# The last stage of a two-layer graph kernel: written order, output in dead buffers, seven input buffers

## The chip, the cores and the metric

The kernel runs on one core of one Trainium2 chip. The metric is device time in microseconds (us) of one execution. The kernel before takes 2909.42 us (median of three runs, 2908.18 to 2910.81); the profiled execution spans 2908.0 us. The engines are called by the names the profile gives them: PE is the matrix engine (PEld its weight loads), DVE the vector engine, ACT the scalar engine, POOL is GpSimd, SP the engine that here only issues transfers. A batch means one of the 16 slices of the input, 1024 rows of 256 numbers, 1 MB in float32.

## The reference, cut to what matters

Two layers, each of which adds the output of a graph network to its input and normalises every row. Only the end of layer 1 is touched.

```python
def _layernorm(x, axis=-1, eps=1e-5):
    m = jnp.mean(x, axis=axis, keepdims=True)
    v = jnp.var(x, axis=axis, keepdims=True)
    return (x - m) / jnp.sqrt(v + eps)

def _L1_gnn_ref(features, A, W1, b1, g1, be1, W2, b2, g2, be2):
    # ... A_hat = the normalised adjacency
    agg = jnp.einsum('nm,bmd->bnd', A_hat, features)
    x = agg.reshape(-1, d)
    h = jax.nn.relu(_batchnorm(x @ W1.T + b1, g1, be1))
    out = h @ W2.T + b2
    out = _batchnorm(out, g2, be2)      # statistics over all 16 x 1024 rows, per feature
    return out.reshape(b, n, -1)

# x: (16, 1024, 256), float32
x = _layernorm(x + _L0_gnn_ref(x, ...), axis=-1)      # layer 0, not touched here
x = _layernorm(x + _L1_gnn_ref(x, adj, ...), axis=-1) # layer 1
```

The second batch norm needs statistics over all batches, so nothing of the last stage can start until the last matrix product with `W2` has been measured. The stage then does, for every batch: scale and shift each feature, transpose back from feature-major to row-major, add the input of the layer (called x1), take mean and variance of each row, normalise, store.

## The kernel before

The stage before the last one computes `h @ W2.T` for every batch and keeps all 16 results in SBUF, feature-major, in the tiles `o2T` (128 features x 2 x 1024 rows). x1 was written to DRAM by layer 0 and is read back into the tiles `xf`, of which there are three (`fin`, `bufs=3`). The tiles `hl` (two of 2 MB) hold the operand of the product.

```python
ps_t = ctx.enter_context(tc.tile_pool(name="ps_t", bufs=2, space=PSUM))   # tile_t: 128 x 512
ps_o = ctx.enter_context(tc.tile_pool(name="ps_o", bufs=2, space=PSUM))   # tile_o: 128 x 512
mhalf = const.tile([P, NCH], F32, name="mhalf")                           # all -0.5

def rsqrt(dst, src, eps):                       # lines 577 and 579
    n = dst.shape[1]
    if eps:
        nc.gpsimd.tensor_scalar(dst, src, eps, None, ALU.add)
        src = dst
    nc.gpsimd.tensor_tensor(dst, src, mhalf[:, :n], ALU.pow)
# ... cut: layer 0 and the first part of layer 1
with (
    tc.tile_pool(name="o2p", bufs=1) as o2p,
    tc.tile_pool(name="fin", bufs=3) as fin,
):
    o2T = [o2p.tile([P, CC, N], F32, tag=f"o2_{b}", name=f"o2_{b}") for b in range(B)]
    xf = {}
    def load_x1(b):                             # transfer at line 1086
        xf[b] = fin.tile([P, NCH, C], F32, tag="xf", name=f"xf_{b}")
        nc.sync.dma_start(xf[b], x1_d[b])

    with tc.tile_pool(name="hl", bufs=2) as hl:
        # ... cut: per batch, load hl, relu and scale on ACT, product into o2T (lines 1092 to 1107),
        #     bn_stats of o2T into bn2_st (line 1111)
            if b >= B - 3:
                load_x1(b - (B - 3))            # x1 of batches 0, 1, 2

    sg2, sh2 = batchnorm_coeffs(bn2_st, cols["g2"], cols["be2"], CC, "bn2")

    def residual2(b):
        for c in range(CC):                     # CC = 2
            o = o2T[b][:, c, :]
            nc.scalar.activation(o, o, AF.Identity, bias=sh2[:, c : c + 1],
                                 scale=sg2[:, c : c + 1])            # line 1123
        xt = xf[b]
        st = small.tile([P, NCH, 6], F32, tag="ln_st", name=f"st_l1_{b}")
        mv = small.tile([P, NCH, 2], F32, tag="ln_mv", name=f"mv_l1_{b}")
        for pair in range(NCH // 2):            # NCH = 8
            pt = tile_t(f"pf_{b}_{pair}")
            for j in range(2):
                n = 2 * pair + j
                for c in range(CC):
                    nc.tensor.transpose(
                        pt[:, j * C + c * P : j * C + (c + 1) * P],
                        o2T[b][:, c, n * P : (n + 1) * P], ident)    # line 1134
            xs = xt[:, 2 * pair : 2 * pair + 2, :].rearrange("p n c -> p (n c)")
            nc.vector.tensor_add(xs, pt, xs)                         # line 1139
            for n in (2 * pair, 2 * pair + 1):
                nc.vector.bn_stats(st[:, n, :], xt[:, n, :])         # line 1141
                nc.vector.bn_aggr(mv[:, n, :], st[:, n, :])          # line 1142
        rstd = small.tile([P, NCH], F32, tag="ln_rs", name=f"rs_l1_{b}")
        rsqrt(rstd, mv[:, :, 1], EPS)
        nmr = small.tile([P, NCH], F32, tag="ln_nm", name=f"nm_l1_{b}")
        nc.vector.scalar_tensor_tensor(nmr, mv[:, :, 0], -1.0, rstd,
                                       op0=ALU.mult, op1=ALU.mult)   # line 1146
        return rstd, nmr

    def finish(b, rstd, nmr):
        xt = xf.pop(b)
        for n in range(NCH):
            nc.scalar.activation(xt[:, n, :], xt[:, n, :], AF.Identity,
                bias=nmr[:, n : n + 1], scale=rstd[:, n : n + 1])    # line 1154
        nc.gpsimd.dma_start(out[b].rearrange("(n p) c -> p n c", p=P), xt)  # line 1158

    before = None
    for b in range(B):
        if b not in xf:
            load_x1(b)
        now = residual2(b)
        if before is not None:
            finish(b - 1, *before)
        before = now
    finish(B - 1, *before)
```

Within an engine the compiler's scheduler chooses the order of these instructions. In the kernel before, ACT does the scaling of batches 0 to 4 in one row, then the first normalisation, and so on.

Of the kernel before, what the change touches and what calls it, by code (L numbers as in the profile page):

```python
# [10 lines left out]
F32 = mybir.dt.float32  # L11
I32 = mybir.dt.int32
AF = mybir.ActivationFunctionType
ALU = mybir.AluOpType
# [4 lines left out]
P = 128  # L19
HALF = 512  # L20
EPS = 1e-5
# [494 lines left out]
def fast_path(  # L516
# [19 lines left out]
    nc = tc.nc  # L536
    B, N, C = x.shape
    H = 4
    D = C // H
    NCH = N // P  # L540
    CC = C // P
    FH = W1.shape[0]
    HC = FH // P
    scale = float((1.0 + 1e-06) / (np.sqrt(D) + 1e-06))

    const = ctx.enter_context(tc.tile_pool(name="const", bufs=1))
    small = ctx.enter_context(tc.tile_pool(name="small", bufs=4))
# [5 lines left out]
    def tile_s(name):  # L553
        return ps_s.tile([P, N], F32, tag="s", name=name)

    def tile_t(name):
        return ps_t.tile([P, HALF], F32, tag="t", name=name)

    def tile_o(name):
        return ps_o.tile([P, HALF], F32, tag="o", name=name)  # L560
# [6 lines left out]
    ident = const.tile([P, P], F32, name="ident")  # L567
# [3 lines left out]
    mhalf = const.tile([P, NCH], F32, name="mhalf")  # L571
    nc.gpsimd.memset(mhalf, -0.5)

    def rsqrt(dst, src, eps):
# [5 lines that stand above are left out]
# [33 lines left out]
    with (  # L613
# [15 lines left out]
        st = {}  # L629
# [242 lines left out]
        with tc.manual_schedule(engines={mybir.EngineType.PE, mybir.EngineType.Activation, mybir.EngineType.DVE}):  # L872
# [25 lines left out]
            for j in range(len(bursts)):  # L898
                b, u = j // PERB, j % PERB
# [28 lines left out]
            j = len(bursts)  # L928
# [38 lines left out]
    with (  # L967
# [34 lines left out]
        for m in range(NCH):  # L1002
            for half in range(2):
                pt = tile_t(f"pah_{m}_{half}")
# [53 lines left out]
    def batchnorm_coeffs(stats, gamma, beta, k, name):  # L1058

        mv = const.tile([P, k, 2], F32, name=f"{name}_mv")  # L1060
        sg = const.tile([P, k], F32, name=f"{name}_sg")
        sh = const.tile([P, k], F32, name=f"{name}_sh")
        for j in range(k):
            nc.vector.bn_aggr(mv[:, j, :], stats[:, j].rearrange("p a s -> p (a s)"))
        rsqrt(sg, mv[:, :, 1], EPS)
        nc.vector.tensor_mul(sg, sg, gamma)
        nc.vector.tensor_mul(sh, mv[:, :, 0], sg)
        nc.vector.tensor_sub(sh, beta, sh)
        return sg, sh
# [5 lines left out]
# [4 lines that stand above are left out]
        o2T = [  # L1079
            o2p.tile([P, CC, N], F32, tag=f"o2_{b}", name=f"o2_{b}") for b in range(B)  # L1080
        ]
        xf = {}

        def load_x1(b):
            xf[b] = fin.tile([P, NCH, C], F32, tag="xf", name=f"xf_{b}")
            nc.sync.dma_start(xf[b], x1_d[b])

        with tc.tile_pool(name="hl", bufs=2) as hl:
            sg1, sh1 = batchnorm_coeffs(bn1_st, cols["g1"], cols["be1"], HC, "bn1")
            for b in range(B):  # L1090
                ht = hl.tile([P, HC, N], F32, tag="hl", name=f"hl_{b}")
                nc.sync.dma_start(ht, h_d[b])
                for k in range(HC):
                    nc.scalar.activation(  # L1094
                        ht[:, k, :], ht[:, k, :], AF.Relu,
                        bias=sh1[:, k : k + 1], scale=sg1[:, k : k + 1],
                    )
                for c in range(CC):
                    ps = tile_s(f"po2_{b}_{c}")
                    for k in range(HC):  # L1100
                        for half in range(2):
                            hs = slice(half * HALF, (half + 1) * HALF)
                            nc.tensor.matmul(  # L1103
                                ps[:, hs], w2T[:, k, c * P : (c + 1) * P], ht[:, k, hs],
                                start=(k == 0), stop=(k == HC - 1),
                            )
                    nc.vector.tensor_scalar(
                        o2T[b][:, c, :], ps, cols["b2"][:, c : c + 1], None, ALU.add
                    )
                    for half in range(2):  # L1110
                        nc.vector.bn_stats(
                            bn2_st[:, c, 2 * b + half, :],
                            o2T[b][:, c, half * HALF : (half + 1) * HALF],
                        )
                if b >= B - 3:
                    load_x1(b - (B - 3))

        sg2, sh2 = batchnorm_coeffs(bn2_st, cols["g2"], cols["be2"], CC, "bn2")

        def residual2(b):  # L1120
            for c in range(CC):
                o = o2T[b][:, c, :]
                nc.scalar.activation(
                    o, o, AF.Identity, bias=sh2[:, c : c + 1], scale=sg2[:, c : c + 1]
                )
            xt = xf[b]
            st = small.tile([P, NCH, 6], F32, tag="ln_st", name=f"st_l1_{b}")
            mv = small.tile([P, NCH, 2], F32, tag="ln_mv", name=f"mv_l1_{b}")
            for pair in range(NCH // 2):
                pt = tile_t(f"pf_{b}_{pair}")  # L1130
                for j in range(2):
                    n = 2 * pair + j
                    for c in range(CC):
                        nc.tensor.transpose(
                            pt[:, j * C + c * P : j * C + (c + 1) * P],
                            o2T[b][:, c, n * P : (n + 1) * P], ident,
                        )
                xs = xt[:, 2 * pair : 2 * pair + 2, :].rearrange("p n c -> p (n c)")
                nc.vector.tensor_add(xs, pt, xs)
                for n in (2 * pair, 2 * pair + 1):  # L1140
                    nc.vector.bn_stats(st[:, n, :], xt[:, n, :])
                    nc.vector.bn_aggr(mv[:, n, :], st[:, n, :])
            rstd = small.tile([P, NCH], F32, tag="ln_rs", name=f"rs_l1_{b}")
            rsqrt(rstd, mv[:, :, 1], EPS)
            nmr = small.tile([P, NCH], F32, tag="ln_nm", name=f"nm_l1_{b}")
            nc.vector.scalar_tensor_tensor(
                nmr, mv[:, :, 0], -1.0, rstd, op0=ALU.mult, op1=ALU.mult
            )
            return rstd, nmr

        def finish(b, rstd, nmr):
            xt = xf.pop(b)
            for n in range(NCH):
                nc.scalar.activation(  # L1154
                    xt[:, n, :], xt[:, n, :], AF.Identity,
                    bias=nmr[:, n : n + 1], scale=rstd[:, n : n + 1],
                )
            nc.gpsimd.dma_start(out[b].rearrange("(n p) c -> p n c", p=P), xt)  # L1158

        before = None  # L1160
        for b in range(B):
            if b not in xf:
                load_x1(b)
            now = residual2(b)
            if before is not None:
                finish(b - 1, *before)
            before = now
        finish(B - 1, *before)

def kernel(tc: tile.TileContext, *args):


    with tc.tile_pool(name="flag", bufs=1, space=DRAM) as flag:
        good_d = flag.tile([1, 1], I32, name="good_d")
        fast_path(tc, *args, good_d)
        good = tc.nc.values_load(good_d[0:1, 0:1], min_val=0, max_val=2 * P)  # L1179
        with tc.If(good < 2 * P):  # L1180
            general_path(tc, *args)
# [30 lines left out]
```

## Time and profile before

| what | value |
|---|---|
| time, median of three | 2909.42 us |
| span of the profiled execution | 2908.0 us |
| last matrix product ends, last statistics | about 2743 us |
| first scaling of the last stage on ACT (line 1123) | 2745.93 us |
| last normalisation on ACT (line 1154) begins, its 8 instructions take | 2895.33 us, 4.04 us |
| end of span | 2908.0 us |
| store of one batch (line 1158), median from issue to landing | 5.6 us |
| transfers in the last stage | 13 loads of x1 and 16 stores, 1024 KB each |

The profile gives the start of an instruction or of a run of like instructions ("x8"), how long it ran, and in brackets how long its engine sat idle before it and what ended that idle time ("<-DMA xf<-x" is the arrival of an x1 load). A table by stretches gives, for each engine, busy time and in brackets the number of instructions, then the clock that the matrix engine was granted, the busy share of the 16 transfer engines and the rate they moved.

### The profile page before, as it was taken

Reading aid. Unit: us, or ns where it says so; the run is one execution under the profiler, and the core shown is the slowest. Engines: PE = TensorE matmul, PEld = TensorE weight load, DVE = VectorE, ACT = ScalarE, POOL = GpSimd, SP = SyncE. Lnnn points to the kernel's source line nnn. Section 1 sums busy time; section 2 is a strip of 40 time slices with the busy share of each in tenths; the row PEclk is TensorE's granted clock in tenths of the full one; section 3 lists DMA queues with packets and bytes.
Section 4 is the critical chain, followed back from the end, with each engine's and each line's share of the span. In section 5 each row is a group of like instructions: output and inputs, shape, how many; then the busy total and the mean of one; then the engine's idle time right before and its main releaser. Section 6 shows DMA issues by size and latency. Waiting matters only on the chain. (4 is left out here: it accounts for less than half of the span.)

```text
span 2908.0 us, 32691 instructions
## 1 busy us (share of the span) xinstructions
PE 2702.1 (93%) x13522; PEld 1200.7 (41%) x13522; DVE 1444.5 (50%) x2130; ACT 1138.5 (39%) x1313; POOL 185.8 (6%) x196
## 2 busy tenths in 40 slices
PE   5899999999999999999999998799999999999842
PEld 2344443444444444444443446444444444344332
DVE  2456666656656756765765655411112112333464
ACT  2444644554553653653563542010111001233473
POOL 0000000000000000100000001000000000000032
PEclk8899999999999999999999997799999999999955
DMA  4001011011011101101101011022121111334165
GB/s 130 8 8 30 9 37 30 9 36 38 16 23 37 30 9 37 30 8 37 30 9 38 16 51 39 15 87 116 72 87 68 76 73 58 130 145 161 70 222 199
DMA packets 122062, 169.00 MB, mean 58 GB/s; under 512 B 86704, under 2 KB 103600, under 8 KB 111664
## 3 DMA queue, kind: packets, MB, share of 16 engines
q1 hardware_dynamic: 112720, 99.70, 11.3%
q0 software_dynamic: 9184, 67.12, 5.9%
q8 instruction: 108, 1.77, 0.3%
q14 instruction: 50, 0.41, 0.0%
HBM read 99.36 MB, written 67.44 MB: 57 GB/s over the span
## 5 line engine op out<-in xcount | busy, mean ns | idle before, releaser
L779 ACT ACTIVATE p<-ps 128x1024 f32<-128x1024 f32 x512 | 495.0, 1019 | 151.9 <-PE ps L774 82.8
L774 PE MATMUL ps<-qT,kT 64*64 64x512 f32 x4096 | 496.4, 599 | 12.1 <-ACT p L779 12.1
L795 PE MATMUL po<-p,v 64*64 64x512 f32 x4096 | 486.9, 589 | 0.0
L804 DVE TENSOR_TENSOR acc<-acc,p 128x1024 f32<-128x1024 f32 x384 | 469.9, 1224 | 26.0 <-ACT p L779 3.5
L700 PE MATMUL pg<-wg,x 128*128 128x512 f32 x1024 | 451.4, 594 | 1.6 <-ACT kT L721 1.6
L1024 PE MATMUL pagg<-ahT,x1l 128*128 128x512 f32 x1024 | 444.1, 593 | 0.0
L1043 ACT ACTIVATE hw<-ph,col_b 128x1024 f32<-128x1024 f32 x64 | 71.3, 1114 | 657.1 <-PE ph L1039 657.1
L1024 PEld LDWEIGHTS pagg<-ahT,x1l 128*128 128x128 f32 x1024 | 194.4, 191 | 241.1 <-issue 241.1
L700 PEld LDWEIGHTS pg<-wg,x 128*128 128x128 f32 x1024 | 189.7, 190 | 231.9 <-issue 216.5
L795 PEld LDWEIGHTS po<-p,v 64*64 64x64 f32 x4096 | 162.6, 133 | 277.8 <-issue 277.1
L774 PEld LDWEIGHTS ps<-qT,kT 64*64 64x64 f32 x4096 | 148.9, 133 | 299.9 <-issue 225.8
L709 ACT ACTIVATE qT<-qT 128x512 f32<-128x512 f32 x64 | 40.4, 631 | 529.8 <-DVE qT L706 529.8
L1103 PE MATMUL po<-hl,w2T 128*128 128x512 f32 x512 | 222.8, 598 | 6.9 <-ACT hl L1094 6.9
L1028 DVE COPY agg<-pagg 128x1024 f32<-128x1024 f32 x32 | 39.2, 1225 | 377.8 <-PE pagg L1024 377.8
L1039 PE MATMUL ph<-agg,w1T 128*128 128x512 f32 x512 | 222.2, 592 | 0.0
L688 DVE SCALAR_TENSOR_TENSOR wg<-wg,adj_s 128x1024 f32<-128x1024 f32 x128 | 170.9, 1353 | 50.1 <-ACT wg L684 50.1
L706 DVE SCALAR_TENSOR_TENSOR qT<-pg,para_s 128x512 f32<-128x512 f32 x64 | 44.2, 690 | 259.5 <-PE pg L700 259.5
L850 POOL TENSOR_TENSOR x<-x,o 128x512 f32<-128x512 f32 x64 | 81.0, 1266 | 1418.3 <-DVE o L845 1418.3
L730 PE MATMUL pv<-kvw_s,xT 128*128 128x256 f32 x512 | 127.0, 393 | 35.3 <-DVE v L734 25.5
L1045 DVE BATCH_NORM_STATS2 bn_st<-hw 128x6 f32<-128x512 f32 x128 | 82.4, 685 | 152.3 <-ACT hw L1043 152.3
L679 ACT ACTIVATE wg<-crow,ccol 128x1024 f32<-128x1024 f32 x128 | 147.4, 1151 | 16.7 <-DMA crow<-c 16.6
L1103 PEld LDWEIGHTS po<-hl,w2T 128*128 128x128 f32 x512 | 98.3, 192 | 131.4 <-issue 121.9
(87 smaller groups left out, 2034.9 us busy)
## 6 DMA issues: line engine op xcount, KB each, us to landing
h<-hw POOLq DMA_DIRECT2D x16, 2048.0 KB, 6.6
hl<-h SPq DMA_DIRECT2D x16, 2048.0 KB
x<-in_x_dram SPq DMA_DIRECT2D x16, 1024.0 KB
x<-x POOLq DMA_DIRECT2D x16, 1024.0 KB, 4.2
x1l<-x SPq DMA_DIRECT2D x16, 1024.0 KB
xf<-x SPq DMA_DIRECT2D x16, 1024.0 KB
out_dram<-xf POOLq DMA_DIRECT2D x16, 1024.0 KB, 5.6
crow<-c SPq DMA_DIRECT2D x16, 512.0 KB
```

Source lines behind the costliest of these rows:

```text
L679: nc.scalar.activation(w, s["crow"], AF.Abs, bias=s["ccol"][:, n : n + 1])
L688: nc.vector.scalar_tensor_tensor(w, w, 1.0, adj_s[:, n, :], op0=ALU.subtract, op1=ALU.mult)
L700: nc.tensor.matmul(ps, xt[:, n, c * P : (c + 1) * P], s["wg", n][:, hs], start=(n == 0), stop=(n == NCH - 1),)
L730: nc.tensor.matmul(pt[:, j * C : (j + 1) * C], s["xT"][:, c, n * P : (n + 1) * P], kvw_s[:, c, C : 2 * C], start=(c == 0), stop=(c == CC - 1),
L774: nc.tensor.matmul(ps[kh * D : (kh + 1) * D, hd * HALF : (hd + 1) * HALF], kT[r, pr, ks], qT[r, pr, qh * HALF : (qh + 1) * HALF], start=Tr ...
L779: nc.scalar.activation(p, ps, AF.Exp)
L795: nc.tensor.matmul(g["po"][kh][hd * D : (hd + 1) * D, :], s["v"][r, m, h * D : (h + 1) * D], p[r, hd * HALF : (hd + 1) * HALF], start=(m = ...
L804: nc.vector.tensor_add(g["acc"], g["acc"], p)
L1024: nc.tensor.matmul(ps[:, hs], xt[:, m, c * P : (c + 1) * P], ahT[:, m, hs], start=(m == 0), stop=(m == NCH - 1),)
L1039: nc.tensor.matmul(ps[:, hs], w1T[:, c, k * P : (k + 1) * P], t[:, c, hs], start=(c == 0), stop=(c == CC - 1),)
L1045: nc.vector.bn_stats(bn1_st[:, k, 2 * b + half, :], ht[:, k, half * HALF : (half + 1) * HALF])
L1103: nc.tensor.matmul(ps[:, hs], w2T[:, k, c * P : (c + 1) * P], ht[:, k, hs], start=(k == 0), stop=(k == HC - 1),)
```

## The change

Four things are changed, all in the last stage. First, PE, ACT and DVE follow the order of the program text there (`manual_schedule`), and the text is arranged so that the scaling of a batch comes a batch ahead of its use. Second, the normalised rows are written into `o2T[b]`, which nobody reads any more once the batch has been transposed, and not in place; the store reads from there, and is issued on SP. So an `xf` tile comes free when the normalisation has read it, not when the store has landed. Third, there are four more `xf` tiles (`fin2`), in the space that `hl` leaves, seven in all. Fourth, the mean and variance are no longer put together by `bn_aggr` on DVE: ten small GpSimd instructions on all eight row groups at once compute the two coefficients from the raw statistics (even and odd elements have mean and summed square deviation each). The transposes use both pairs of PSUM tiles in turn.

```diff
-        def load_x1(b):
-            xf[b] = fin.tile([P, NCH, C], F32, tag="xf", name=f"xf_{b}")
+        def load_x1(b, pool):
+            xf[b] = pool.tile([P, NCH, C], F32, tag="xf", name=f"xf_{b}")
             nc.sync.dma_start(xf[b], x1_d[b])
 ... cut
+        with (
+            tc.tile_pool(name="fin2", bufs=4) as fin2,
+            tc.manual_schedule(
+                engines={mybir.EngineType.PE, mybir.EngineType.Activation, mybir.EngineType.DVE}
+            ),
+        ):
+            for b in range(3, 7):
+                load_x1(b, fin2)
+            def scale_shift(b):
+                for c in range(CC):
+                    o = o2T[b][:, c, :]
+                    nc.scalar.activation(
+                        o, o, AF.Identity, bias=sh2[:, c : c + 1], scale=sg2[:, c : c + 1]
+                    )
             def residual2(b):                      # scaling taken out of it
-                pt = tile_t(f"pf_{b}_{pair}")
+                pt = tile_t(f"pf_{b}_{pair}") if pair % 2 else tile_o(f"pf_{b}_{pair}")
                 ... transposes, tensor_add, bn_stats as before
-                    nc.vector.bn_aggr(mv[:, n, :], st[:, n, :])
-            rsqrt(rstd, mv[:, :, 1], EPS)
-            nc.vector.scalar_tensor_tensor(
-                nmr, mv[:, :, 0], -1.0, rstd, op0=ALU.mult, op1=ALU.mult
-            )
+                me, qe, mo, qo = (st[:, :, k] for k in (1, 2, 4, 5))
+                w = small.tile([P, 4, NCH], F32, tag="ln_w", name=f"w_l1_{b}")
+                rstd, nmr, dif, var = (w[:, k, :] for k in range(4))
+                pool = nc.gpsimd
+                pool.tensor_tensor(nmr, me, mo, ALU.add)
+                pool.tensor_tensor(dif, me, mo, ALU.subtract)
+                pool.tensor_tensor(var, qe, qo, ALU.add)
+                pool.tensor_scalar(var, var, 1.0 / C, EPS, ALU.mult, ALU.add)
+                pool.tensor_tensor(dif, dif, dif, ALU.mult)
+                pool.tensor_scalar(dif, dif, 0.25, None, ALU.mult)
+                pool.tensor_tensor(var, var, dif, ALU.add)
+                pool.tensor_tensor(rstd, var, mhalf, ALU.pow)
+                pool.tensor_tensor(nmr, nmr, rstd, ALU.mult)
+                pool.tensor_scalar(nmr, nmr, -0.5, None, ALU.mult)
+                return rstd, nmr
             def finish(b, rstd, nmr):
                 xt = xf.pop(b)
+                y = o2T[b].rearrange("p c n -> p (c n)").rearrange("p (n c) -> p n c", c=C)
                 for n in range(NCH):
                     nc.scalar.activation(
-                        xt[:, n, :], xt[:, n, :], AF.Identity,
+                        y[:, n, :], xt[:, n, :], AF.Identity,
                         bias=nmr[:, n : n + 1], scale=rstd[:, n : n + 1],
                     )
-            nc.gpsimd.dma_start(out[b].rearrange("(n p) c -> p n c", p=P), xt)
+                nc.sync.dma_start(out[b].rearrange("(n p) c -> p n c", p=P), y)
+                if b + 7 < B:
+                    load_x1(b + 7, fin if b < 3 else (fin2 if b < 7 else fin))
+            scale_shift(0)
+            coeffs = {}
+            for b in range(B):
+                coeffs[b] = residual2(b)
+                if b + 1 < B:
+                    scale_shift(b + 1)
+                if b:
+                    finish(b - 1, *coeffs.pop(b - 1))
+            finish(B - 1, *coeffs.pop(B - 1))
```

In the compiled program the instructions of every engine are in the same order as before up to this stage. In it, ACT's order is scaling of 0, 1, 2, normalisation of 0, scaling of 3, normalisation of 1, and so on to scaling of 15, normalisation of 13, 14, 15. The loads of x1 for batches 3 to 6 wait on PE and ACT (the last use of `hl`), and each later load stands on SP behind the store of the batch whose buffer it takes.

More of the change, by code (lines that the diff above doesn't have):

```diff
@@ L1115, in fast_path @@
                 if b >= B - 3:
-                    load_x1(b - (B - 3))
+                    load_x1(b - (B - 3), fin)
         sg2, sh2 = batchnorm_coeffs(bn2_st, cols["g2"], cols["be2"], CC, "bn2")
[L1120 to L1124, printed above, removed]
-                )
[L1126 to L1129, printed above, removed]
-                pt = tile_t(f"pf_{b}_{pair}")
[L1131 to L1143, printed above, removed]
-            rsqrt(rstd, mv[:, :, 1], EPS)
-            nmr = small.tile([P, NCH], F32, tag="ln_nm", name=f"nm_l1_{b}")
-            nc.vector.scalar_tensor_tensor(
-                nmr, mv[:, :, 0], -1.0, rstd, op0=ALU.mult, op1=ALU.mult
-            )
-            return rstd, nmr
@@ L1151, in finish @@
[L1151 to L1154, printed above, removed]
-                    xt[:, n, :], xt[:, n, :], AF.Identity,
[L1156 to L1167, printed above, removed]
@@ L1168, in fast_path, with residual2, finish @@
-        finish(B - 1, *before)
+        with (
[12 more added lines that the diff above has]
+                    )
+            def residual2(b):
+                xt = xf[b]
+                st = small.tile([P, NCH, 6], F32, tag="ln_st", name=f"st_l1_{b}")
+                for pair in range(NCH // 2):
+                    pt = tile_t(f"pf_{b}_{pair}") if pair % 2 else tile_o(f"pf_{b}_{pair}")
+                    for j in range(2):
+                        n = 2 * pair + j
+                        for c in range(CC):
+                            nc.tensor.transpose(
+                                pt[:, j * C + c * P : j * C + (c + 1) * P],
+                                o2T[b][:, c, n * P : (n + 1) * P], ident,
+                            )
+                    xs = xt[:, 2 * pair : 2 * pair + 2, :].rearrange("p n c -> p (n c)")
+                    nc.vector.tensor_add(xs, pt, xs)
+                    for n in (2 * pair, 2 * pair + 1):
+                        nc.vector.bn_stats(st[:, n, :], xt[:, n, :])
+                me, qe, mo, qo = (st[:, :, k] for k in (1, 2, 4, 5))
[13 more added lines that the diff above has]
+                return rstd, nmr
+            def finish(b, rstd, nmr):
+                xt = xf.pop(b)
+                y = o2T[b].rearrange("p c n -> p (c n)").rearrange("p (n c) -> p n c", c=C)
+                for n in range(NCH):
+                    nc.scalar.activation(
+                        y[:, n, :], xt[:, n, :], AF.Identity,
+                        bias=nmr[:, n : n + 1], scale=rstd[:, n : n + 1],
+                    )
+                nc.sync.dma_start(out[b].rearrange("(n p) c -> p n c", p=P), y)
[10 more added lines that the diff above has]
+            finish(B - 1, *coeffs.pop(B - 1))
```

## The prediction

> **What bounds the kernel now.** The slices of the page show PE at nine tenths nearly throughout; only in the last stage (after 2745) is it half idle. So I cut that stage into stretches of 10 us, to see whether any engine is full:
>
> ```profile
> core 0: us, PE busy (x) PEld busy (x) DVE busy (x) ACT busy (x) POOL busy (x), PEclk, DMA share, GB/s
> 2765.00:2775.00 10.00, 3.82 (x16) 3.14 (x16) 5.68 (x21) 10.00 (x19) 3.54 (x5) 0.50 0.73 265
> 2775.00:2785.00 10.00, 3.08 (x14) 2.61 (x14) 5.04 (x18) 8.40 (x13) 2.63 (x4) 0.50 0.90 324
> 2815.00:2825.00 10.00, 4.64 (x20) 3.47 (x18) 6.76 (x27) 4.58 (x9) 1.90 (x2) 0.50 0.69 245
> 2845.00:2855.00 10.00, 2.51 (x11) 2.14 (x12) 4.32 (x15) 2.71 (x6) 1.91 (x2) 0.50 0.56 219
> ```
>
> ACT is full early, while it runs ahead with scaling. From 2815 on no engine is full, and the transfers aren't either. The stage waits; the order of time says for what (start, length, engine, line; in brackets the idle time before):
>
> ```profile
> 2835.99 4.04 ACT L1154 ACTIVATE xf<-xf,nm_l,rs_l 128x256 f32<-128x256 f32 x8 [4.56 <-issue]
> 2840.34 0.96 POOL L1158 DMA_DIRECT2D out_dram<-xf  x1 [4.63 <-ACT xf L1154]
> 2841.60 5.10 SPq L1086 DMA_DIRECT2D xf<-x  x2
> ...
> 2849.13 0.69 DVE L1139 TENSOR_TENSOR xf<-pf,xf 128x512 f32<-128x512 f32 x1 [4.61 <-DMA xf<-x]
> ...
> 2850.01 0.23 POOL L577 TENSOR_SCALAR rs_l<-mv_l 128x8 f32<-128x8 f32 x1 [8.72 <-DVE mv_l L1142]
> 2850.33 1.67 POOL L579 TENSOR_TENSOR rs_l<-rs_l,mhalf 128x8 f32<-128x8 f32 x1
> 2852.04 0.17 DVE L1146 SCALAR_TENSOR_TENSOR nm_l<-mv_l,rs_l 128x8 f32<-128x8 f32 x1 [1.55 <-POOL rs_l L579]
> ```
>
> Two things. A load of x1 is issued at 2841.60 and its add starts at 2849.13: with three tiles a load waits for a store to land, so normalise, store, load, add stand in one ring. And POOL waits 8.72 us for the means of a batch whose adds were over at 2843: in the scheduler's order its last `bn_aggr` stands behind the first add of the next batch, and so behind that load. ACT idles 12.26 us before the normalisation at 2852.29. The cost of each operation is in the groups of the last stage:
>
> ```profile
> L1154 ACT ACTIVATE xf<-xf,nm_l,rs_l 128x256 f32<-128x256 f32 x128 | 64.5, 587 | 52.8 <-issue 42.9 <-DVE nm_l L1146 9.3 <-ACT xf L1154 0.6
> L1141 DVE BATCH_NORM_STATS2 st_l<-xf 128x6 f32<-128x256 f32 x128 | 48.8, 405 | 0.0
> L1139 DVE TENSOR_TENSOR xf<-pf,xf 128x512 f32<-128x512 f32 x64 | 42.0, 669 | 28.0 <-DMA xf<-x 20.3 <-SPq L1180 4.2 <-PE pf L1134 3.4
> L1123 ACT ACTIVATE o<-o,bn_sh,bn_sg 128x1024 f32<-128x1024 f32 x32 | 36.9, 1226 | 20.2 <-POOL bn_sg L579 20.2
> L579 POOL TENSOR_TENSOR rs_l<-rs_l,mhalf 128x8 f32<-128x8 f32 x16 | 26.7, 1669 | 1.3
> L1142 DVE BATCH_NORM_AGGREGATE mv_l<-st_l 128x2 f32<-128x6 f32 x128 | 21.0, 168 | 0.0
> ```
>
> **What the Trainium skill says.** "Perfetto Trace Analysis", section "DVE / Act Engine Instruction (TENSOR_ADD, Activation, etc)": a slice includes the acknowledgement of the write, and the next instruction may start before that. The trace agrees: 16 normalisations in a row take 7.96 us, so (7.96 - 0.585)/15 = 0.49 us apart, though one lasts 0.585. "VectorE: DVE Perf Modes", section "The DRAIN you can't avoid": an instruction that reads what the one before it wrote on the same engine still needs a semaphore. The trace: statistics of `o2T` start 1.32 us after the 1.28 us eviction whose result they read, while independent adds start 0.57 to 0.66 apart. "GPSIMD Engine Reference", section "1. Specifications": GpSimd shares its SBUF interfaces with DVE, with contention when DVE is in a two-port mode or has two SBUF inputs. Here the adds have one input in PSUM and the statistics have one input, and the trace shows no contention: the small GpSimd operation takes 232 to 253 ns, the add 654 to 692. "DMA: Bandwidth & Descriptors", section "Issuing engines are not separate DMA queues": all issuing engines feed the same 16 transfer engines. So stores on SP in place of GpSimd bring no rate; the trace before can't show it, as stores stand on one engine there.
>
> **The change part by part.** All engines have the same instruction order as before up to 2745.93, so only the 2908.0 - 2745.9 = 162.1 us of the last stage can move.
>
> ACT: the count doesn't change. A batch has two scalings, 1.13 us apart ((11.43 - 1.226)/9 in the first row of ten) = 2.27, and eight normalisations at 0.494 = 3.95: 6.22 us, for 16 batches 99.5. Most normalisations now also wait on PE and DVE for the buffer they write; those waits are long met, and I allow 1.5 us in all.
>
> DVE: 128 `bn_aggr` (21.0 us) and 16 of line 1146 (2.7) go. In written order each pair is add, 0.70 us until its dependent statistics, then two statistics 0.33 apart: 1.36; four pairs 5.44 us a batch. That is less than ACT's 6.22.
>
> POOL: the 16 store issues (15.2 us) and the old 0.24 + 1.67 go; ten operations come. Nine at 0.33 from start to start (0.24 and the 0.08 the trace has between line 577 and its dependent line 579; an add of 512 elements takes 1.27 us, line 850, so eight elements add nearly nothing) and the power at 1.7: 4.7 us a batch, under 6.22, but in the chain.
>
> PE: 16 transposes in 3.94 us a batch at half clock. With four PSUM tiles it can be a batch ahead. Not a limit.
>
> Transfers: the first seven loads no longer wait on a store. The loads of batches 3 to 6 go when `hl` is free, at about 2740; 4.2 MB at 400 GB/s is there by 2751, and batch 3 is added at about 2767. Later loads have over five batches (30 us) of time. In nine batches both a load and a store run, 2.1 MB in 6.22 us = 337 GB/s, just what the transfers reached before (324 at 0.90 busy is 360 when full); behind them come seven batches with a store alone, 169 GB/s, in which a lag is made up. Hidden.
>
> Ramp: scaling of batch 0 ends at 2748.3; PE's first tile 1.2 us later; DVE 5.44; POOL 4.7; 0.2 of passing on: first normalisation at 2759.9. ACT has by then done three scalings (to 2752.8) and idles 7.1 us. In the steady state scaling to normalisation takes 1.2 + 5.5 + 4.7 + 0.2 = 11.6 us, and ACT has 2 x 6.22 = 12.4 us of other work between, so it doesn't wait. At the end only two normalisations (7.9) stand between the last scaling and the last normalisation: 3.7 us idle.
>
> Sum: 2745.9 + 99.5 + 1.5 + 7.1 + 3.7 = 2857.7 for the end of ACT. Before, ACT ended at 2899.4 and the span at 2908.0, 8.6 us for the last store and the close; I keep 8.5. Span 2866.2, and with the 1.4 between the span and the median of before, 2867.6. I say **2867 us**, 42 less or 1.5%.
>
> **The rivals.** GpSimd becomes the bound: if the nine small operations take 0.6 each (raw statistics are read with a stride, each waits for the one before), a batch takes 7.1 us there, and 2755.1 + 16 x 7.1 + 4 + 8.5 gives a span of 2881, a time of 2883. Against it: 32 operations of that shape at 0.24. The transfers become the bound: nothing shows 1 KB stores issued by SP; at 250 GB/s loads and stores together, the 26.2 MB that remain from 2764 on take 105 us and end at 2869, with the close a time of 2875. For it: line 1158 writes rows of 1 KB. Against it: loads of x from the input have the same 1 KB rows and reach 385 GB/s. A third: the store of the last batch is quicker from SP and the waits cost nothing, 2863.
>
> **Range and chances.** Even with ACT never idle the span would be 2745.9 + 99.5 + 8.5 = 2853.9, a time of 2855; 2% less than before is 2851.2. So faster by over 2% needs an ACT instruction to become shorter: 0.03. Slower by over 2% would need a rival of over 100 us: 0.01. Within 2%: 0.96. The range reaches from the third rival with a little less ramp, 2858, to between the other two, 2880.
>
> **What would show it.** Right: ACT full from 2760 to the end in the stretches, 6.2 to 6.4 us from one normalisation to the next, one idle time of 7 us at the start and one of 4 before the last; no DVE wait on an x1 load after batch 2; POOL about 75 us busy in the stage, and never waited for but at both ends. Wrong: ACT idle before each normalisation with POOL as the cause; adds that wait for loads; stores that end long after ACT.

## The result, and the profile after

The changed kernel takes 2862.19 us (median of four runs, 2860.24 to 2862.41) beside 2909.93 for the kernel before (median of four as well, 2908.18 to 2910.81): a ratio of 0.9835, with the interval 0.9818 to 0.9852. The profiled span is 2860.5 us after 2908.0. Both kernels reach the last stage within 0.7 us of each other (its first scaling starts at 2745.21, before at 2745.93), so nearly the whole gain lies there. I call the time from the first scaling to the end of the span the **stage length**: 162.1 us before, 115.3 after. It leaves out that the part ahead of the stage ends sooner or later from run to run (the first scaling starts between 2742.20 and 2746.82 in the profiles below), and the experiments are compared by it as well as by the medians. It comes from one profiled execution each. Ratios are to the kernel before as measured beside each group of runs; its medians there are 2907.68 to 2909.93, so medians of different groups that lie within 2 us of each other are not told apart.

The same stretches as before, now of the changed kernel (columns as there):

```profile
core 0: us, PE busy (x) PEld busy (x) DVE busy (x) ACT busy (x) POOL busy (x), PEclk, DMA share, GB/s
2765.00:2775.00 10.00, 6.05 (x31) 5.05 (x29) 9.07 (x20) 10.00 (x19) 6.63 (x19) 0.67 1.02 332
2785.00:2795.00 10.00, 5.76 (x26) 4.64 (x24) 9.10 (x21) 10.00 (x17) 5.88 (x15) 0.63 1.00 346
2815.00:2825.00 10.00, 6.78 (x30) 5.69 (x28) 8.74 (x19) 10.00 (x18) 6.71 (x20) 0.50 0.76 259
2835.00:2845.00 10.00, 4.38 (x23) 3.39 (x21) 9.35 (x22) 9.50 (x17) 5.73 (x14) 0.67 0.41 137
```

ACT is full, where in the kernel before it was 2.7 to 4.6 tenths busy after 2815. DVE is close behind, and the transfer engines are full in the first half: a share of 1.00 or more at 332 to 346 GB/s. ACT in order of time:

```profile
2745.21 6.91 ACT L1135 ACTIVATE o<-o,bn_sh,bn_sg 128x1024 f32<-128x1024 f32 x6 [20.18 <-POOL bn_sg L579]
2758.27 4.06 ACT L1176 ACTIVATE o<-xf,w_l 128x256 f32<-128x256 f32 x8 [6.15 <-POOL w_l L1169]
2762.24 2.36 ACT L1135 ACTIVATE o<-o,bn_sh,bn_sg 128x1024 f32<-128x1024 f32 x2
2764.50 4.05 ACT L1176 ACTIVATE o<-xf,w_l 128x256 f32<-128x256 f32 x8
...
2836.84 2.36 ACT L1135 ACTIVATE o<-o,bn_sh,bn_sg 128x1024 f32<-128x1024 f32 x2
2839.11 4.04 ACT L1176 ACTIVATE o<-xf,w_l 128x256 f32<-128x256 f32 x8
2843.66 4.06 ACT L1176 ACTIVATE o<-xf,w_l 128x256 f32<-128x256 f32 x8 [0.50 <-POOL w_l L1169]
2849.68 4.05 ACT L1176 ACTIVATE o<-xf,w_l 128x256 f32<-128x256 f32 x8 [1.97 <-POOL w_l L1169]
```

Three idle times are all there is: 6.15 us before the first normalisation, 0.50 and 1.97 before the last two. Between 2758.27 and 2839.11 there are 13 batches, 6.22 us each. The groups of the stage say that no add waits for a load any more:

```profile
L1176 ACT ACTIVATE o<-xf,w_l 128x256 f32<-128x256 f32 x128 | 64.7, 588 | 8.6 <-POOL w_l L1169 8.6
L1154 DVE BATCH_NORM_STATS2 st_l<-xf 128x6 f32<-128x256 f32 x128 | 48.2, 418 | 3.0
L1152 DVE TENSOR_TENSOR xf<-pf,xf 128x512 f32<-128x512 f32 x64 | 43.4, 677 | 10.0 <-PE pf L1147 5.5 <-issue 4.5
L1135 ACT ACTIVATE o<-o,bn_sh,bn_sg 128x1024 f32<-128x1024 f32 x32 | 37.6, 1228 | 20.2 <-POOL bn_sg L579 20.2
L1167 POOL TENSOR_TENSOR w_l<-w_l,mhalf 128x8 f32<-128x8 f32 x16 | 26.7, 1666 | 1.3
```

The adds (line 1152) idled 28.0 us before, 20.3 of it on loads; now 10.0, none of it. Normalisations (line 1176) idled 52.8, now 8.6. The busy times of the groups that stayed are within 4% of those of before: nothing became faster in itself. The coefficients of one batch on POOL (two of the ten lines left out):

```profile
2754.28 0.21 POOL L1160 TENSOR_TENSOR w_l<-st_l 128x8 f32<-128x8 f32 x1 [9.74 <-DVE st_l L1154]
2754.45 0.20 POOL L1161 TENSOR_TENSOR w_l<-st_l 128x8 f32<-128x8 f32 x1
...
2754.79 0.19 POOL L1164 TENSOR_TENSOR w_l<-w_l 128x8 f32<-128x8 f32 x1
2755.07 0.20 POOL L1163 TENSOR_SCALAR w_l<-w_l 128x8 f32<-128x8 f32 x1
2755.34 0.26 POOL L1165 TENSOR_SCALAR w_l<-w_l 128x8 f32<-128x8 f32 x1
2755.69 0.20 POOL L1166 TENSOR_TENSOR w_l<-w_l 128x8 f32<-128x8 f32 x1
2755.97 1.67 POOL L1167 TENSOR_TENSOR w_l<-w_l,mhalf 128x8 f32<-128x8 f32 x1
...
2758.00 0.24 POOL L1169 TENSOR_SCALAR w_l<-w_l 128x8 f32<-128x8 f32 x1
```

The first four start 0.17 us apart. After the fourth, each starts 0.27 to 0.35 after the one ahead, except for the one behind the power, which starts 1.74 after it. From the first to the end of the last is 3.96 us, and 0.03 us later ACT starts. The view of the transfers in 40 slices of 3.15 us (2735 to 2861; busy tenths, then rate):

```profile
DMA  0299910009999999999999998997273636369090
GB/s 0 44 367 421 429 70 0 0 2 304 364 307 362 309 369 299 378 291 389 297 382 295 364 317 336 336 358 276 96 239 112 226 117 221 125 213 319 30 331 5
```

The loads of batches 3 to 6, alone on the transfer engines at 421 to 429 GB/s, are over in the sixth slice, by 2754 at the latest. From the first store at 2762 the transfers are full, or nearly, for some 55 us; ACT is full as well, and waits for none of them.

### The profile page after: what moved, and what is told of

Read it like the earlier page. It is cut to its first block, busy times and chain, and to the rows that moved or that the text cites. A ratio compares the mean times of both kernels' runs of the same rounds, so it can differ in the third digit from the quotient of the medians.

```text
span 2860.5 us, 32692 instructions
## 1 busy us (share of the span) xinstructions
PE 2696.9 (94%) x13522; PEld 1198.0 (42%) x13522; DVE 1438.2 (50%) x1986; ACT 1138.4 (40%) x1313; POOL 195.0 (7%) x308
## 4 chain that ended last, share of the span: by engine, by line
PE 73%; DVE 13%; ACT 7%; issue 4%; DMA 2%; POOL 1%; ACTq 0%; DVEq 0%; POOLq 0%; SPq 0%
PE pagg L1024 15%; PE pg L700 12%; PE ps L774 11%; PE po L795 10%; PE po L1103 8%; PE ph L1039 8%; DVE acc L804 4%; PE pk L717 3%; PE pv L730 2%; ACT p L779 2%; DVE x L590 1%; DVE st_l L586 1%; ACT o L1176 1%; DMA c<-ncol 1%; ACT wg L679 1%
```

## The experiments

Three theories stood at the start. **A, the ring:** with three tiles written in place, normalise, store, load, add stand in one ring, and breaking it (more tiles, or another place for the output) is the gain. **B, the order:** what the written order brings (no `bn_aggr` behind an add that waits for a load, scaling a batch ahead) is the gain. **C, DVE's relief:** the gain needs the 21 us of `bn_aggr` taken off DVE.

**More tiles alone, in the kernel before.** Everything else stays: in place, the scheduler's order, `bn_aggr`.

```diff
+        with tc.tile_pool(name="fin2", bufs=4) as fin2:
+            for b in range(3, 7):
+                load_x1(b, fin2)
... the loop as before, but its loads into
+                    load_x1(b, fin2 if 10 <= b < 14 else fin)
```

> The kernel before with seven x1 tiles and nothing else of the change (in place, stores on GpSimd, bn_aggr on DVE, scheduler's order). Theory A (the gain is the broken ring store-load-add): most of the gain, 2872 to 2885 us, adds no longer wait for loads. Theory B (the gain is the written order): 2900 or more. Theory C (the gain is the relief of DVE by GpSimd): 2890 or more.

2870.51 us (2870.24 to 2872.16), ratio 0.9870 [0.9853, 0.9886]; stage length 124.8, so 37.3 of the 46.8 us. The groups of this kernel:

```profile
L1154 ACT ACTIVATE xf<-xf,nm_l,rs_l 128x256 f32<-128x256 f32 x128 | 64.6, 587 | 15.4 <-DVE nm_l L1146 15.4
L1139 DVE TENSOR_TENSOR xf<-pf,xf 128x512 f32<-128x512 f32 x64 | 42.1, 658 | 3.5 <-PE pf L1134 3.4
```

The wait on loads is gone from the adds with nothing but more tiles. A holds; B and C can't be the main cause. ACT still idles 15.4 us, on the coefficients that DVE finishes at line 1146.

**Written order alone, in the kernel before.**

```diff
+        with tc.manual_schedule(
+            engines={mybir.EngineType.PE, mybir.EngineType.Activation, mybir.EngineType.DVE}
+        ):
             before = None
             for b in range(B):
... the rest of the loop as before
```

> The kernel before with PE, ACT and DVE in written order and nothing else. Theory A: the ring stays, and DVE now stands still about 2.2 us a batch for GpSimd's power in front of line 1146 (6.9 + 2.3 = 9.2 us a batch, about what the kernel before takes): 2895 to 2915 us. Theory B: 2880 or less.

2913.98 us (2912.55 to 2916.3), ratio 1.0021 [1.0013, 1.0029]: slower by 0.2%; stage length 168.5, so 6.4 longer. The adds' group, and DVE in order of time, at the boundary of two batches:

```profile
L1139 DVE TENSOR_TENSOR xf<-pf,xf 128x512 f32<-128x512 f32 x64 | 42.6, 666 | 3.6 <-PE pf L1134 3.5
2838.24 0.18 DVE L1142 BATCH_NORM_AGGREGATE mv_l<-st_l 128x2 f32<-128x6 f32 x1
2840.54 0.17 DVE L1146 SCALAR_TENSOR_TENSOR nm_l<-mv_l,rs_l 128x8 f32<-128x8 f32 x1 [2.12 <-POOL rs_l L579]
2840.72 0.69 DVE L1139 TENSOR_TENSOR xf<-pf,xf 128x512 f32<-128x512 f32 x1
```

In written order line 1146 stands between a batch's last `bn_aggr` and the next batch's first add, and DVE stands still for POOL's power each time. A batch takes 9.53 us here (line 1146 at 2831.01 and at 2840.54), of which 7.2 are DVE at work. No add waits for a load: at this pace the loads come in time. B falls for this text: its order takes a wait on loads away and puts a wait on POOL in its place. The text of the change, which scales a batch ahead, is tried without its order below.

**The change with three tiles.** Output into `o2T` and the rest stay.

```diff
-            tc.tile_pool(name="fin2", bufs=4) as fin2,
...
-            for b in range(3, 7):
-                load_x1(b, fin2)
...
-                if b + 7 < B:
-                    load_x1(b + 7, fin if b < 3 else (fin2 if b < 7 else fin))
+                if b + 3 < B:
+                    load_x1(b + 3, fin)
```

> The changed kernel with three x1 tiles in place of seven. Theory A: normalise 4.0, store and load behind each other on the same transfer engines 7.3, adds and statistics 5.5, coefficients 4.0, passing on 0.3: 21.1 us for three batches, 7.0 a batch against 6.2, so 2868 to 2878 us, and DVE waits on loads. Rival (four more tiles are what the gain is): 2895 or more.

2879.17 us (2877.47 to 2879.94), ratio 0.9901 [0.9884, 0.9917]; stage length 132.8. A batch takes 7.42 us, not 7.0 (from the normalisation of batch 2, at 2768.41, to that of batch 15, at 2864.89), so I missed by a little over 1 us at the upper edge. The group of the adds:

```profile
L1149 DVE TENSOR_TENSOR xf<-pf,xf 128x512 f32<-128x512 f32 x64 | 43.3, 676 | 27.8 <-DMA xf<-x 23.9 <-PE pf L1144 3.9
```

A load stands on SP behind the store that was issued just ahead of it, and the two share the transfer engines. From the end of a normalisation to the add that takes its buffer over I had assumed 7.3 us; the trace has 7.85 for batch 3 (2781.69 to 2789.54) and 9.45 for batch 4 (2788.02 to 2797.47).

**The change, output in place, with seven tiles and with three.** The first has only the line of `y`; the second has it and the edit before.

```diff
-                y = o2T[b].rearrange("p c n -> p (c n)").rearrange("p (n c) -> p n c", c=C)
+                y = xt
```

> The changed kernel, but normalised in place: the store reads the x1 tile, so a load waits until a store has landed; seven tiles. Theory A: with seven tiles the ring is 4.0 + 6 + 7 + 5.5 + 4.0 = 26.5 us over seven batches, 3.8 a batch, no bound: 2860 to 2865 us. Rival (the dead buffers are what breaks the ring): 2880 or more.

> The changed kernel with three tiles and in place: the ring of the kernel before in the new order. Theory A: 4.0 + 5.7 landing + 5.1 load + 5.5 + 4.0 + 0.3 = 24.6 us for three batches, 8.2 a batch, 2882 to 2900 us. Theory B (order) or C (GpSimd coefficients): 2870 or less.

With seven tiles 2862.74 us (2861.78 to 2863.61), stage length 115.5: no different from the change. With three tiles 2897.58 (2896.16 to 2900.19), ratio 0.9962 [0.9948, 0.9976], stage length 151.7, at 8.84 us a batch (again from batch 2 to batch 15) where I expected 8.2. Its adds:

```profile
L1149 DVE TENSOR_TENSOR xf<-pf,xf 128x512 f32<-128x512 f32 x64 | 43.3, 677 | 46.3 <-DMA xf<-x 22.3 <-ACT xf L1173 20.5 <-PE pf L1144 3.4
```

So the two ways to loosen the ring act on the same wait. With three tiles the dead buffer is worth 151.7 - 132.8 = 18.9 us, about half of what four more tiles bring there (151.7 - 115.5 = 36.2); with seven tiles it is worth nothing. Everything in the change but the ring is worth 162.1 - 151.7 = 10.4 us, and the tiles alone 37.3: together 47.7, near the 46.8 of the whole. Among the rest is that the transposes use both pairs of PSUM tiles in turn; that was not tried by itself.

**The change without written order.**

```diff
-            tc.manual_schedule(
-                engines={mybir.EngineType.PE, mybir.EngineType.Activation, mybir.EngineType.DVE}
-            ),
```

> The changed kernel without the written order: the scheduler orders PE, ACT and DVE. In the compiled order ACT has nine scalings before the first normalisation in place of six, the rest is nearly the same. Theory A: the same or up to 3 us less, 2858 to 2863 us. Theory B: 2880 or more.

2856.93 us (2855.52 to 2858.88), ratio 0.9822 [0.9805, 0.9838]; stage length 110.9: 4.4 us shorter than the change, 1 us below the lower end expected. ACT's first two rows here:

```profile
2746.08 10.30 ACT L1132 ACTIVATE o<-o,bn_sh,bn_sg 128x1024 f32<-128x1024 f32 x9 [20.30 <-POOL bn_sg L579]
2758.68 4.04 ACT L1173 ACTIVATE o<-xf,w_l 128x256 f32<-128x256 f32 x8 [2.30 <-POOL w_l L1166]
```

The scheduler puts nine scalings ahead of the first normalisation, the written order six. From the first scaling to the first normalisation it is nearly as long (12.6 us, 13.1 in the change); more of it is filled: 2.30 us idle for 6.15. None of the gain hangs on the written order; with the ring broken, this order as it stands costs time.

**`bn_aggr` back on DVE, in the change.** POOL keeps the power and three small operations.

```diff
                         nc.vector.bn_stats(st[:, n, :], xt[:, n, :])
+                        nc.vector.bn_aggr(mv[:, n, :], st[:, n, :])
... the ten POOL operations become
+                rsqrt(rstd, mv[:, :, 1], EPS)
+                nc.gpsimd.tensor_tensor(nmr, mv[:, :, 0], rstd, ALU.mult)
+                nc.gpsimd.tensor_scalar(nmr, nmr, -1.0, None, ALU.mult)
```

> The changed kernel with bn_aggr back on DVE (each right behind its bn_stats) and four small GpSimd operations for the two coefficients. DVE then takes per pair 0.70 + 0.45 + 0.08 + 0.45 + 0.08 = 1.76, 7.0 us a batch, over ACT's 6.2: DVE is the bound, 2870 to 2878 us. Rival (DVE has room, the move did nothing): 2860 to 2863. Rival C (the move made the whole gain): 2890 or more.

2880.88 us (2878.35 to 2881.08), ratio 0.9900 [0.9884, 0.9917]; stage length 132.7, so 17.4 more than the change; the time is 2.9 us over the upper end that I expected. ACT now waits in every batch:

```profile
2839.06 4.04 ACT L1169 ACTIVATE o<-xf,w_l 128x256 f32<-128x256 f32 x8 [0.93 <-POOL w_l L1162]
2843.00 2.36 ACT L1135 ACTIVATE o<-o,bn_sh,bn_sg 128x1024 f32<-128x1024 f32 x2
2846.29 4.04 ACT L1169 ACTIVATE o<-xf,w_l 128x256 f32<-128x256 f32 x8 [0.93 <-POOL w_l L1162]
```

7.23 us a batch (2839.06 to 2846.29) is DVE's time: four pairs of add, two statistics and two aggregates, each behind the one that it reads. C holds in a weaker form: the move is worth 17 us once the ring is broken and the order fixed. By itself, in the kernel before, it wasn't tried. The run with more tiles alone, also with `bn_aggr` on DVE, has 124.8: there the scheduler sets a statistic or an add between a statistic and its aggregate, so that DVE doesn't stand. From that run to the change without written order, 124.8 to 110.9, are 13.9 us, of which the move is one part among several.

**A second power on POOL, its result thrown away.**

```diff
+                pool.tensor_tensor(dif, var, mhalf, ALU.pow)
                 pool.tensor_tensor(rstd, var, mhalf, ALU.pow)
```

> The changed kernel with the power on GpSimd done twice (the first result is thrown away), 1.75 us more in each batch's chain. By my step of the ramp and the steady state: scaling to coefficients 10.7 becomes 12.4 us, just what ACT's other work covers (12.4), so only both ends pay, 2863 to 2868 us. Rival (GpSimd stands in the path of every batch): 16 x 1.75 = 28 more, 2890.

2865.63 us (2864.48 to 2867.89), ratio 0.9851 [0.9835, 0.9868]; 3.4 us more by the medians and 3.8 by the stage length (119.1), for 16 x 1.67 = 26.7 us more of POOL's work. It shows at both ends:

```profile
2759.77 4.04 ACT L1177 ACTIVATE o<-xf,w_l 128x256 f32<-128x256 f32 x8 [7.77 <-POOL w_l L1170]
...
2847.16 4.04 ACT L1177 ACTIVATE o<-xf,w_l 128x256 f32<-128x256 f32 x8 [2.17 <-POOL w_l L1170]
2853.36 4.04 ACT L1177 ACTIVATE o<-xf,w_l 128x256 f32<-128x256 f32 x8 [2.16 <-POOL w_l L1170]
```

1.62 us at the start (7.77 for 6.15) and 1.86 at the end (4.33 for 2.47). In between, next to nothing: the 13 batches from 2759.77 to 2840.94 take 6.24 us each, for 6.22. POOL lies in the chain of a batch, but ACT has other batches to do. GpSimd as the bound falls.

**Stores on GpSimd again, in the change.**

```diff
-                nc.sync.dma_start(out[b].rearrange("(n p) c -> p n c", p=P), y)
+                nc.gpsimd.dma_start(out[b].rearrange("(n p) c -> p n c", p=P), y)
```

> The changed kernel with the stores issued on GpSimd, as before. From the end of the last normalisation to the end of the span there were 8.6 us before and 6.8 after; if it is the issuing engine: 8.6 again, 1 to 3 us more, 2863 to 2866 us. GpSimd has 0.95 us more in each batch, which the steady state hides. Rival (the tail doesn't depend on it): 2860 to 2863.

2867.89 us (2866.59 to 2870.43), ratio 0.9858 [0.9843, 0.9873]; stage length 120.3; 2 us over what I expected. From ACT's last normalisation to the end of the span is 2866.1 - 2857.43 = 8.7 us here, 2860.5 - 2853.73 = 6.8 in the change; that part came as expected. The other was not foreseen:

```profile
2768.15 4.04 ACT L1176 ACTIVATE o<-xf,w_l 128x256 f32<-128x256 f32 x8 [3.02 <-POOL w_l L1169]
```

On POOL the store of batch 0 stands ahead of the coefficients of batch 1 and waits for ACT to finish batch 0; ACT then waits 3.02 us for those coefficients, once. Later batches have the slack for it.

**Scaling three batches ahead.** ACT then has the scalings of five batches, and not of three, to fill its first wait with.

```diff
-            scale_shift(0)
+            for b in range(3):
+                scale_shift(b)
...
-                if b + 1 < B:
-                    scale_shift(b + 1)
+                if b + 3 < B:
+                    scale_shift(b + 3)
```

> The changed kernel with the scaling three batches ahead in the text and not one: ACT does it in the 6.2 us in which it idles before the first normalisation, and has less to do before the last. If ACT is the bound: 5 to 7 us less, 2855 to 2858 us. Rival (the transfers, which are busy all the time between 2765 and 2815, are the bound): no change, 2860 to 2863.

2856.47 us (2856.1 to 2856.94), ratio 0.9818 [0.9804, 0.9831]; stage length 107.8. ACT's first two rows and its last:

```profile
2746.82 11.43 ACT L1135 ACTIVATE o<-o,bn_sh,bn_sg 128x1024 f32<-128x1024 f32 x10 [19.95 <-POOL bn_sg L579]
2759.88 4.04 ACT L1176 ACTIVATE o<-xf,w_l 128x256 f32<-128x256 f32 x8 [1.63 <-POOL w_l L1169]
...
2828.07 19.75 ACT L1176 ACTIVATE o<-xf,w_l 128x256 f32<-128x256 f32 x40
```

One idle time of 1.63 us is left, and the last five batches are one row of 40: ACT's work alone sets this stage, and the transfers, though full, don't. Against the change without written order this is no clear gain: the medians are 2856.47 and 2856.93. What can still go is work of ACT's.

**With it, one normalisation in eight on GpSimd.**

```diff
... y as in finish, ahead of the return of the coefficients
+                pool.tensor_scalar(y[:, 7, :], xt[:, 7, :], rstd[:, 7:8], nmr[:, 7:8],
+                                   ALU.mult, ALU.add)
... in finish, on ACT
-                for n in range(NCH):
+                for n in range(NCH - 1):
```

> As the last, and one of the eight normalisations of a batch on GpSimd. ACT falls to 5.7 us a batch, DVE has 5.5. If an operation of 256 elements takes GpSimd about 0.5 us: DVE and ACT end together, 2851 to 2856 us. Rival (GpSimd and DVE get in each other's way, or the transfers are the bound): 2857 or more.

2853.97 us (2853.1 to 2855.39), ratio 0.9809 [0.9795, 0.9822]; stage length 106.9. ACT's batch fell by 0.49 to 5.71 us, which over 16 is 7.8, but the stage gave 0.9 and the median 2.5 (the profiled run is the slowest of the five). Of ACT's rows, the last:

```profile
2837.59 3.55 ACT L1182 ACTIVATE o<-xf,w_l 128x256 f32<-128x256 f32 x7 [2.03 <-POOL w_l L1169]
2843.16 3.55 ACT L1182 ACTIVATE o<-xf,w_l 128x256 f32<-128x256 f32 x7 [2.03 <-POOL w_l L1169]
```

5.57 us apart, and 2.03 idle each time: this is DVE's pace, four pairs at 1.38 and a little at the boundary. As long as ACT also has scalings to do, its batch of 5.71 is longer; the last four batches have none, and there ACT has caught up with DVE, which from its first add on has 3.0 us of idle time in the whole stage. I took DVE for the bound; the next run tests it.

**With both, each pair's statistics behind the add of the next pair.**

```diff
+                def stats(pair):
+                    for n in (2 * pair, 2 * pair + 1):
+                        nc.vector.bn_stats(st[:, n, :], xt[:, n, :])
...
                     nc.vector.tensor_add(xs, pt, xs)
-                    for n in (2 * pair, 2 * pair + 1):
-                        nc.vector.bn_stats(st[:, n, :], xt[:, n, :])
+                    if pair:
+                        stats(pair - 1)
+                stats(NCH // 2 - 1)
```

> As the last but one (scaling three ahead, one normalisation of eight on GpSimd), with DVE's statistics of a pair moved behind the add of the next pair, so that no statistics follow directly on the add whose result they read. If DVE was the bound there (5.6 us a batch, ACT waiting 2.03 us before each of the last normalisations): DVE falls to 4 x (0.60 + 2 x 0.33) = 5.1, ACT's 5.7 is the bound again, 1.6 + 16 x 5.7 + 6.8 = 99.7 us for the stage in place of 106.9: 2845 to 2850 us. Rival (the wait was GpSimd's own chain, or the transfers bound it): 2852 to 2855.

2846.29 us (2844.71 to 2846.49), ratio 0.9786 [0.9772, 0.9799]; stage length 99.7. The fastest kernel here, 16 us under the change. DVE in order of time, first in the run before, then in this one:

```profile
2801.35 0.67 DVE L1152 TENSOR_TENSOR xf<-pf,xf 128x512 f32<-128x512 f32 x1
2802.06 0.75 DVE L1154 BATCH_NORM_STATS2 st_l<-xf 128x6 f32<-128x256 f32 x2
2802.73 0.67 DVE L1152 TENSOR_TENSOR xf<-pf,xf 128x512 f32<-128x512 f32 x1
```

```profile
2799.55 0.68 DVE L1156 TENSOR_TENSOR xf<-pf,xf 128x512 f32<-128x512 f32 x1
2800.14 0.74 DVE L1144 BATCH_NORM_STATS2 st_l<-xf 128x6 f32<-128x256 f32 x2
2800.80 0.68 DVE L1156 TENSOR_TENSOR xf<-pf,xf 128x512 f32<-128x512 f32 x1
```

Statistics that read an older result start 0.59 us after the add; in the run before, where they read that add's own result, 0.71 to 0.78. A pair takes 1.25 us and not 1.38. The Trainium skill says in "VectorE: DVE Perf Modes", section "The DRAIN you can't avoid", that after an operation DVE waits for its pipeline to empty, but that a next operation which isn't held back starts earlier; the trace agrees, with a start 0.59 us after an add that lasts 0.68. The faster pace took 7.2 us off the stage, so DVE was the bound in the run before, and neither POOL's chain nor the transfers. ACT's first two rows and its last, and one stretch:

```profile
2744.06 11.43 ACT L1135 ACTIVATE o<-o,bn_sh,bn_sg 128x1024 f32<-128x1024 f32 x10 [20.13 <-POOL bn_sg L579]
2756.88 3.55 ACT L1187 ACTIVATE o<-xf,w_l 128x256 f32<-128x256 f32 x7 [1.39 <-POOL w_l L1174]
...
2819.68 17.29 ACT L1187 ACTIVATE o<-xf,w_l 128x256 f32<-128x256 f32 x35
```

```profile
2795.00:2805.00 10.00, 7.22 (x35) 5.05 (x33) 10.00 (x25) 10.00 (x16) 8.02 (x23) 0.68 1.03 359
```

Once started, ACT never waits; DVE and ACT are both full, POOL eight tenths, and the transfers full at 359 GB/s.

## Why the prediction was right

The mechanism was right in what carried the sum: the waits that the ring had caused go, and ACT is what holds the stage now. Of the two causes that the prediction read from the trace, the ring is shown to be the main one. The other, the last `bn_aggr` behind the first add of the next batch, can't be: more tiles alone leave it there (the add at 2804.67, the `bn_aggr` at 2805.24), and 37.3 of the 46.8 us go. The time was 5 us under the predicted 2867 and inside the range. In the order of the prediction's sum:

| term | predicted | measured | how |
|---|---|---|---|
| first scaling of the stage | 2745.9 | 2745.2 | ACT's first row |
| ACT's work and its satisfied waits | 99.5 + 1.5 | 99.9 | 2745.21 to 2853.73, less 8.62 idle |
| idle before the first normalisation | 7.1 | 6.15 | its row |
| idle before the last ones | 3.7 | 2.47 | 0.50 + 1.97 |
| last store and close | 8.5 | 6.8 | 2853.73 to 2860.5 |
| median over span | 1.4 | 1.7 | 2862.19 - 2860.5 |

- **The waits on PE and DVE before each normalisation** were allowed 1.5 us and cost nothing that shows: a batch of two scalings and eight normalisations takes 6.22 us with them, as reckoned without them.
- **The two idle times** were too long by 2.2 us together, mostly because of "nine at 0.33" on POOL: the first four operations start 0.17 us apart, the later small ones 0.27 to 0.35. The coefficients take 3.96 us and not 4.7, which is 0.74 in each idle time, 1.5 of the 2.2; the rest isn't traced to a term. The run with a second power shows both idle times following POOL's time nearly one to one.
- **The close** was the largest miss, 1.7 us: I kept the 8.6 of before. The run with stores back on GpSimd has 8.7, so the shorter close belongs to the issue on SP. Both things that the third rival named, a quicker store and waits that cost nothing, came true, and its 2863 is close. But they make only 1.7 + 1.1 us of the 5.4 between the sum's 2867.6 and the time; the shorter idle times, which it did not name, make 2.2, and the stage began 0.7 sooner (0.3 go the other way in the last row). That its number fits so well is in part luck.
- **DVE** came at 1.38 us a pair (2799.57 to 2800.95), 1.36 predicted. **POOL** is 55 us busy in the stage, not 75: the coefficients take 16 x 3.96 = 63 us from start to end, and the gaps between the operations, which the 0.33 had counted, are not busy time.
- **The chain of a batch** was put at 11.6 us of 12.4 available. For batch 3, from the end of its scaling (2762.24 + 2.36 = 2764.60) to its coefficients at 2775.27, the trace has 10.7. It was right that the steady state has slack; the second power used 1.67 of it unseen.
- **The transfers** were "hidden", and are, but nearer to the edge than the words say. 337 GB/s were needed; from 2765 to 2815 the share is at or about 1.00, at about that rate. The prediction counted only on later batches to make up a lag. The runs that do more in less time (99.7 us of stage length) still don't wait on them, at 359 GB/s. The rival that stores issued by SP in rows of 1 KB would hold the transfers to 250 GB/s falls.
- **What the prediction didn't see** is how the four parts stand to each other. It reckoned them all at once, as work and waits of ACT; the runs show limits one behind the other. By batch: the ring about 9.3 us (in the kernel before, eight batches from 2820.67 to 2895.33), then DVE with `bn_aggr` in written order at 7.2, then ACT at 6.2; with one normalisation in eight moved, ACT at 5.7 and DVE at 5.6 close behind it, which shows in the last batches, where ACT has no scalings left. A part brings no more than what lies between its limit and the next. The dead `o2T` buffer is worth nothing beside seven tiles, and the written order, for all its part in the plan, costs 4.4 us of stage length, as its text lets ACT scale only three batches before the first normalisation; with five it is level with the scheduler's order (107.8 and 110.9 in the profiles, medians 2856.47 and 2856.93).

Not settled: the 0.4 and 0.6 us a batch by which the two runs with three tiles came out above what was expected. In the first of them a store and a load take longer together than assumed; no run here parts their order on SP from their sharing of the transfer engines.

## What to carry to other kernels

When a stage has no full engine, look for a buffer ring: number of buffers times the pace of a batch must exceed the time from one use of a buffer to its next, store and load included. Here three tiles at ACT's 6.22 us give 18.7 us, and one turn of the ring took 3 x 8.84 = 26.5 in place, 3 x 7.42 = 22.3 with the output elsewhere; seven tiles give 43.5. More buffers mended it wholly, another place for the output by half, and both together did no more than the buffers. After that, list the pace that each engine could keep and expect a change to bring no more than the distance to the next. A wait at the start of a stage is paid by filling it: let the bound engine run as far ahead as its inputs allow, and, where a run shows that the pair waits, set independent work between an instruction and the one that reads its result.

## What the hardware showed that was not expected

- The last 1 MB store, issued on SP, closes the span 6.8 us after the last normalisation; on GpSimd, 8.6 (before) and 8.7.
- GpSimd's ten operations on 128x8: the first four start 0.17 us apart, later small ones 0.27 to 0.35 behind the one ahead; the power takes 1.67. Dependence alone doesn't explain the two spacings: lines 1163 and 1165 read a result that was finished 0.25 and 0.36 us before they start, and are among the slower ones. The cause is not shown. Its multiply-and-add of 128x256 takes 0.56 us beside a full DVE, whose adds (680 ns) and statistics (416 ns) are as long as without it (677 and 418).
- Stores in rows of 1 KB and loads together filled the transfer engines at 332 to 359 GB/s; loads alone had 421 to 429. The issuing engine changes how the same stores are cut: issued on GpSimd, the 16 of them are 4352 packets for 16.78 MB, and 464 packets of the stage are under 2 KB; issued on SP, 16848 are.
